# Four graph layers in fp32 on one core: the last layer's first matrix in 49 products for pairs of groups, and norms from accumulated sums

## The chip, the core and the metric

The kernel runs on one core of a Trainium2 chip. The metric is the device time of one execution in microseconds. Before the change it is 2160.31 us, the median of three runs (2158.48 to 2162.55). The profile is that of one further execution, whose span is 2156.5 us.

## What is computed

128 graphs of 64 nodes with 512 features pass through four layers. Each ends in x = layernorm(x + layer(x)), everything in fp32. Cut to what matters:

```python
# layer 0: scores s = (x @ w) @ a, A from tanh/exp of s_i + s_j and adj;  out = A @ x @ w
x = _layernorm(x + L0(x, adj, w, a))
# layer 1: weight = adj * exp(q @ k.T), rows normalised;                  out = weight @ v
x = _layernorm(x + L1(x, adj, Wq, Wk, Wv))
# layer 2: softmax over nodes of q . (adj @ k), times v
x = _layernorm(x + L2(x, adj, mask, Wqk, Wv))
# layer 3: two hypergraph convolutions
H = (adj != 0); Dn = 1 / (H @ adj[0]); Be = 1 / H.sum(axis=1)
conv(z, W, b) = Dn * (H @ (Be * (H.T @ (z @ W.T)))) + b
h = _layernorm(relu(conv(x, W1, b1)))      # W1: 1024 x 512
x = _layernorm(x + conv(h, W2, b2) + x)    # W2: 512 x 1024
```

(The last line stands for y + x inside the layer and x + layer(x) outside it.) gamma and beta of the inner norm are ones and zeros in the inputs, but the kernel folds them into W2 and its bias in general.

## The kernel before, in words

**Tiles and groups.** The 8192 nodes are 64 tiles of 128 rows (two graphs each). A group is two tiles, 256 nodes; there are 32 groups (`NG`). `run(g)` at L1005 writes down all steps of one group, 0 to 15: layer 0 in steps 0 to 2, layer 1 in 3 to 6, layer 2 in 7 to 11, layer 3 in 12 to 15. `prepare_chunk` (L700) makes the graph's small matrices for two groups at a time.

**Products by splitting.** A product of a group (256 rows) with a weight matrix is done as a 2x2 splitting with seven products in place of eight (`seven_products`, L849): the left side is cut into four blocks (`left_blocks`, L774), four sums of blocks are made on VectorE (`side_sums`, L829), and the weights exist as seven pieces in the order of `USE` (L488), four blocks and four sums less one that is not needed. Each of the seven results lies in a bank of PSUM; two banks go on accumulating, so that one product follows on the sum of earlier ones. `first` and `more` take a result out: with a scale from a column and added to x (`scaled_into`, L905), or copied. The first matrix of the last layer, called "3a" (512 x 1024), is such a product: the blocks have 128 rows, 256 of depth and 512 columns, so each of the seven products is two matmuls of 128x512 (L1125 to L1140). Its results are scaled, the bias b3a is added and they are summed in h on VectorE; relu follows on ScalarE. The second matrix, "3b" (1024 x 512), has seven products of four matmuls of 128x256 (L1148).

**Weights.** m1 and m2 stay in SBUF. The pieces of the others are computed once at the start, stored in DRAM (`stored_in_place`, L533) and for each group loaded again into the eight tiles of `ring` (`streamed`, L666), in loads of 512 KB.

**Norms.** `normalized` (L924) takes mean and variance of each tile with VectorE's batch statistics (`bn_stats`, `bn_aggr`), adds eps, raises to the power -0.5 on GpSimd, and applies scale and bias on ScalarE. Each group has four of them on x (512 columns) and one on h (1024).

**What sets the order.** No operation is emitted where it is written. `order.add` (L77) collects them with engine, planned cost, what they read and write, and a key. `keys_by_what_follows` (L106) sets the key from the group's place `BASE` (L29), and from the length of what follows in the group. `Order.run` (L141) then plays all engines through with planned costs (`w_pe`, `w_dve`, `w_act`, `w_pool`, L244 to L257) and latencies (`LATENCY`, L60): whenever an engine is free, it takes the ready operation with the lowest key for which buffers are free, and the instruction streams are written in that order. On TensorE, `choose` (L123) groups operations on the whole array and those on a divided array. The kinds of buffers at L299 to L311 bound what can be in flight: six x, fourteen `k4` of 4 KB a row, two h, eight banks, three `product` tokens. Every instruction is emitted through a wrapper, so the profile shows one line, L1177, for nearly all; its groups are told apart by the names of the tiles.

Of the kernel before, what the change touches and what calls it, by code (L numbers as in the profile page):

```python
# [16 lines left out]
P = 128  # L17
B, N, D, DH = 128, 64, 512, 1024
T = B * N // P
GT = 2  # L20
NG = T // GT
CT = 4
# [6 lines left out]
BASE = [APART * g - 2 * min(g, 4) - 2 * max(g - NG + 3, 0) for g in range(NG)]  # L29
# [25 lines left out]
class Op:  # L55
    __slots__ = ("engine", "cost", "emit", "key", "missing", "users", "takes", "touches", "start", "bytes", "step", "mode", "port", "behind", "group", "args", "matmuls")


class Order:
    LATENCY = {"PE": 220, "DVE": 70, "ACT": 60, "POOL": 60, "SP": 2200}  # L60
# [7 lines left out]
    EARLY = [2.22, 0.44, 0.0, 0.0, 0.0, 0.0, 0.0, 0.17, 0.0, 0.57, -0.17, -0.03, -1.1, -0.36, 0.0, -0.35]  # L68

    BLOCK, REST = 64, 3500  # L70
    AHEAD = 3.5

# [4 lines left out]
    def add(self, engine, cost, reads, writes, emit, urgent=0.0, size=0, mode=None, port=False, matmuls=0):  # L77
        o = Op()
        o.engine, o.cost, o.emit, o.key, o.step = engine, cost, emit, self.key - urgent - self.early, self.key
        o.start, o.mode, o.port, o.behind, o.group, o.args, o.matmuls = None, mode, port, None, self.group, (), matmuls  # L80
# [25 lines left out]
    def keys_by_what_follows(self):  # L106

        tail = {}
        for o in reversed(self.ops):
            if o.group is not None:  # L110
                own = 0 if o.engine == "SP" else 2 * o.cost if o.engine == "PE" else o.cost
                tail[o] = own + max((tail[u] + (u.engine != o.engine) * 3 * self.LATENCY[o.engine]
                                     for u in o.users if u.group == o.group), default=0)
        longest = max(tail.values())
        for o in reversed(self.ops):
            if o.group is not None:
                urgent = o.step - o.key
                o.step = BASE[o.group] + STEPS * (1 - tail[o] / longest)
                if o.engine == "SP" and o.users:
                    o.step = min(u.step for u in o.users)  # L120
                o.key = o.step - urgent

# [18 lines left out]
    def run(self):  # L141
# [11 lines left out]
        while len(done) < len(self.ops):  # L153
# [4 lines left out]
            for e, heap in ready.items():  # L158
                while free_at[e] <= now:
# [60 lines left out]
                    for u in found.users:  # L220
                        n += 1
                        heappush(events, (free_at[e] if u.engine == e and e != "SP" else seen, n, u, None))
# [25 lines left out]
def w_dve(n):  # L248
    return 175 + n * 35 // 32


def w_act(n):
    return 175 + n * 27 // 32
# [7 lines left out]
def kernel(  # L261
# [37 lines left out]
    kind("x", 6, GT, D)  # L299
# [7 lines left out]
    kind("k1", 2, CT, N)  # L307
# [3 lines left out]
    kinds["product"] = [None] * 3  # L311
# [12 lines left out]
    def dve(n, reads, writes, emit, urgent=0.0, port=None):  # L324

        if port is None:
            port = all((b[0] if isinstance(b, tuple) else b).kind != "bank" for b in reads)
        order.add("DVE", w_dve(n), reads, writes, emit, urgent, port=port)
# [184 lines left out]
    def in_dram(which, width):  # L513
        n = PIECE // width
        tiles = []
        for i in range(-(-len(USE) // n)):
            tiles.append(const(dram.tile([P, PIECE], FP, name=f"{which}_{i}"), n))
        stored[which] = [(t_, min(n, len(USE) - n * i)) for i, t_ in enumerate(tiles)]

        def store(k, piece):  # L520
            i = USE.index(k)
# [44 lines left out]

    def gram(name, left, right, steps):

        m = const(sb(name, len(USE), 2, D // 2), 2 * len(USE))
# [24 lines left out]
    m1 = gram("m1", wq1_raw, wk1_raw, KC)  # L594
    u1_c = const(sb("u1_c", KC))
# [30 lines left out]
    order.key = 3.0  # L626
    m2 = gram("m2", wq2_raw, wk2_raw, KC // 2)

    order.key = 6.0
# [16 lines left out]
    order.key = 8.0  # L646
    stored_in_place("3a", quarters(w3a), PIECE, PIECE)

    order.key = 10.0
# [16 lines left out]
    def streamed(which, room=()):  # L666

        pieces = []
        chunks = KH // 2 if which == "3b" else KC // 2
        for src, n in stored[which]:  # L670
# [5 lines left out]
                      urgent=1.5, size=P * n * width * 4)  # L676
            for k in range(n):
# [129 lines left out]
    def gathered(tokens, view, right, reads):  # L807
# [4 lines left out]
        def emit(t):  # L812

            for c in range(KC):
                for h, (rows, _) in enumerate(halves):
                    for f, (cols, _) in enumerate(halves):
                        at = (c * GT + t) * N
                        nc.tensor.matmul(ps[h].t[cols, at : at + N], view(t)[rows, c * P + f * N : c * P + f * N + N],
# [29 lines left out]

    def seven_products(a, s, pieces, first, more, across=False):  # L849


        going, pair = Buf("product"), [Buf("bank") for _ in range(2)]
        pieces = iter(pieces)

        def times(ps, left, start=True):
            piece, view = next(pieces)
            token = pair[ps] if isinstance(ps, int) else ps
            chunks = KH // 2 if left[2] else KC // 2
            width = PIECE // chunks if left[2] or wide else D // 2
# [14 lines left out]
            pe(w_pe(P, 2 * chunks) if across else w_pe(width, chunks), [left[0], piece, going], [token], emit,  # L874
# [3 lines left out]
        deep = a["deep"] if "deep" in a else False  # L878
        wide = a["wide"] if "wide" in a else False

        def side(v):
            return v[0], v[1], deep


        first("11", *times(0, side(a["11"])))
        first("22", *times(1, side(s[0])))
        more("11", *times(Buf("bank"), side(a["12"])))
        first("12", *times(0, side(s[1]), False))
        more("12", *times(1, side(s[3]), False))
        first("21", *times(Buf("bank"), side(a["22"])))  # L890
        u = times(0, side(s[2]), False)
        more("22", *u)
        more("21", *u)
# [11 lines left out]
    def scaled_into(at, f, own, n, base=None):  # L905


        def add(k, token, ps, base):
            dst = at[k]
            t = own.start + int(k[0]) - 1  # L910
            dve(n + 40, [*token, f, base[0]], [dst[0]], lambda: nc.vector.scalar_tensor_tensor(
                dst[1](), ps(), f.t[:, t : t + 1], base[1](), ALU.mult, ALU.add), NOW)

        return (lambda k, token, ps: add(k, token, ps, base[k] if base else at[k]),
                lambda k, token, ps: add(k, token, ps, at[k]))
# [8 lines left out]
    def normalized(reads_of, view, n_stats, eps, n, among=range(GT)):  # L924

        m = len(among)
        mv = Buf("col", m)
        for j, t in enumerate(among):
            st = Buf("col", n_stats)
            for i in range(n_stats):  # L930
                dve(n // n_stats, [reads_of(t, i)], [st[i]], lambda t=t, i=i, st=st: nc.vector.bn_stats(
                    st.t[:, 6 * i : 6 * i + 6], view()[:, t, ts(i, n // n_stats)]), port=False)
            dve(12, [st], [mv[j]], lambda j=j, st=st: nc.vector.bn_aggr(mv.t[:, 2 * j : 2 * j + 2], st.t[:, : 6 * n_stats]), port=False)
        ve, rstd, nm = Buf("col"), Buf("col"), Buf("col")

        def pairs_of(b, i):
            return b.t[:, : 2 * m].rearrange("p (t s) -> p t s", s=2)[:, :, i]

        dve(GT, [mv], [ve], lambda: nc.vector.tensor_scalar(ve.t[:, :m], pairs_of(mv, 1), eps, None, ALU.add))
        order.add("POOL", 790, [ve], [rstd],  # L940
                  lambda: nc.gpsimd.tensor_tensor(rstd.t[:, :m], ve.t[:, :m], mhalf[:, :m], ALU.pow), port=True)
        dve(GT, [mv, rstd], [nm], lambda: nc.vector.scalar_tensor_tensor(
            nm.t[:, :m], pairs_of(mv, 0), -1.0, rstd.t[:, :m], ALU.mult, ALU.mult))
        for j, t in enumerate(among):
            for i in range(n_stats):
                act(n // n_stats + 240, [reads_of(t, i), nm, rstd], [reads_of(t, i)], lambda j=j, t=t, i=i: nc.scalar.activation(
                    view()[:, t, ts(i, n // n_stats)], view()[:, t, ts(i, n // n_stats)], AF.Identity,
                    bias=nm.t[:, j : j + 1], scale=rstd.t[:, j : j + 1]))

    def layer_norm(xt, eps=EPS, among=range(GT)):  # L950
        normalized(lambda t, i: xt[[2 * t, 2 * t + 1]], lambda: xt.t, 1, eps, D, among)
# [53 lines left out]
    def run(g):  # L1005
# [9 lines left out]
        of_x = lambda t: xt[[2 * t, 2 * t + 1]], lambda t: xt.t[:, t, :]  # L1015
# [9 lines left out]
        for t in range(GT):  # L1025
# [13 lines left out]
        step(2)  # L1039
        seven_products(*left, first_use["w0"] if g == 0 else streamed("w0"), *scaled_into(  # L1040
            at_x, sums, slice(2 * CT + own.start, 2 * CT + own.stop), D // 2))
        layer_norm(xt)
# [11 lines left out]
        seven_products(*left, m1, *z_into(zT, u1_c), across=True)  # L1054
# [12 lines left out]
        po = [Buf("bank") for _ in range(GT)]  # L1067

# [7 lines left out]
        for t in range(GT):  # L1076
            dve(D + 40, [po[t], f, xt[[2 * t, 2 * t + 1]]], [xt[[2 * t, 2 * t + 1]]],
                lambda t=t: nc.vector.scalar_tensor_tensor(xt.t[:, t, :], po[t].t, f.t[:, t : t + 1], xt.t[:, t, :],
                                                   ALU.mult, ALU.add), NOW)
        layer_norm(xt)  # L1080
# [6 lines left out]
        seven_products(*left, m2, *z_into(zT2), across=True)  # L1087
# [21 lines left out]
        seven_products(*left, streamed("v2"), *scaled_into(at_x, wc, slice(0, GT), D // 2))  # L1109
        layer_norm(xt)  # L1110
# [14 lines left out]
        h = Buf("h", 4)  # L1125
        s3 = Buf("k1")
        a = left_blocks(gT3)
        at_h = block_views(h, lambda: h.t)

        def room(cell, i):  # L1130
            return (h[cell], lambda: h.t[:, cell // 2, ts(cell % 2 * 2 + i, D // 2)].rearrange("p (k q) -> p k q", q=P))

        s_ = [room(1, 0), room(1, 1),
              (s3, lambda: flat(s3.t).rearrange("p (k q) -> p k q", q=P)), room(2, 0)]
# [113 lines left out]
```

## Time and profile before

| what | value |
|---|---|
| median of three runs | 2160.31 us |
| span of the profiled execution | 2156.5 us, 3.8 us under that median |
| TensorE matmul busy | 2139.4 us |
| TensorE weight loads busy | 1721.0 us |
| VectorE, ScalarE, GpSimd busy | 1529.5, 861.1, 385.7 us |
| granted TensorE clock, mean | 0.999 |
| moved by DMA | 476.34 MB, mean 221 GB/s |
| TensorE idle, 0 to 76 us | 9.65 of 76 us |
| TensorE idle, 76 to 2136 us | 0.38 of 2060 us |
| TensorE idle, 2136 us to the end | 7.10 of 20.5 us |
| statistics of x (256 of 128x512) on VectorE | 175.0 us, 689 ns each |
| statistics of h (128 of 128x512) on VectorE | 87.3 us, 686 ns each |
| evictions into h (256 of 128x512) on VectorE | 95.4 + 93.1 us, 746 and 745 ns each |

The page names the engines PE (TensorE's matmuls), PEld (its weight loads), DVE (VectorE), ACT (ScalarE), POOL (GpSimd) and SP (the queue that issues DMAs). A row of digits gives the busy share in 40 slices of the span, in tenths. A group's row has the line, the engine, the operation, the tiles written and read, the shapes, the count, then busy time and the mean duration of one, then the idle time before its instructions and what ended it. Durations of matmuls overlap, so the mean of one is longer than the distance from one to the next; busy time divided by the count, or the distance in the timeline, is what one costs. A timeline row has the start, the length, the engine, the operation and how many instructions were merged.

### The profile page before, as it was taken

The numbers are of one execution on the slowest core, as the hardware profiler recorded it, in microseconds if no ns is written. First come the engines' busy times: TensorE is split into PE (matmuls) and PEld (weight loads), VectorE is DVE, ScalarE is ACT, GpSimd is POOL, SyncE is SP. The second block draws the span as 40 slices with busy tenths as digits, with TensorE's granted clock in tenths as the row PEclk, the third lists the DMA queues.
The fourth block names the chain that finished last, engine by engine and source line by source line (L and its number), as shares of the span: only waits on it lengthen the run. The fifth ranks groups of instructions, "written<-read, shape, count | busy, mean of one in ns | idle before, by whom it ended". The sixth has DMA issues, their size and how long they took to land.

```text
span 2156.5 us, 51432 instructions
## 1 busy us (share of the span) xinstructions
PE 2139.4 (99%) x20829; PEld 1721.0 (80%) x20829; DVE 1529.5 (71%) x3967; ACT 861.1 (40%) x1812; POOL 385.7 (18%) x399
## 2 busy tenths in 40 slices
PE   8999999999999999999999999999999999999998
PEld 4988777787887887878878887888888788888866
DVE  6787767677776676767777776767766777766675
ACT  3444344343343434343443344443434434433343
POOL 1112122011211212111122111212012220112030
PEclk9999999999999999999999999999999999999999
DMA  8775667676666656665666766667666666665576
GB/s 284 268 276 206 229 209 258 227 240 216 218 223 218 207 202 228 220 229 194 211 225 215 228 212 200 215 215 233 220 202 215 221 205 225 213 203 200 171 246 209
DMA packets 174365, 476.34 MB, mean 221 GB/s; under 512 B 35825, under 2 KB 45361, under 8 KB 174129
## 3 DMA queue, kind: packets, MB, share of 16 engines
q1 hardware_dynamic: 174128, 473.05, 66.0%
q8 instruction: 165, 2.70, 0.5%
q14 instruction: 72, 0.58, 0.1%
HBM read 443.33 MB, written 29.66 MB: 219 GB/s over the span
## 4 chain that ended last, share of the span: by engine, by line
PE 97%; DMA 2%; DVE 0%; SPq 0%; ACT 0%; issue 0%; DVEq 0%; ACTq 0%
PE bank L1177 97%; DMA x<-in_x_dram 0%; DMA k<-in_wk_dram 0%; DMA mask_rows<-e 0%; DMA k<-in_wqk_dram 0%; DMA ring<-in_wv_dram 0%; DMA ring<-w 0%; SPq L1177 0%; DVE x L1177 0%; DVE col L1177 0%; DVE ring L1177 0%; ACT x L1177 0%; DVE e L1177 0%; ACT k L1177 0%; DVE k L1177 0%
## 5 line engine op out<-in xcount | busy, mean ns | idle before, releaser
L1177 PE MATMUL bank<-ring,k 128*128 128x256 f32 (+1 forms) x3968 | 1027.7, 409 | 2.3 <-DMA ring<-w 1.5
L1177 PEld LDWEIGHTS bank<-ring,k 128*128 128x128 f32 x3968 | 732.3, 190 | 205.5 <-issue 115.0
L1177 ACT COPY k<-bank 128x512 f32<-128x512 f32 (+1 forms) x640 | 304.3, 501 | 599.0 <-PE bank L1177 513.3
L1177 DVE SCALAR_TENSOR_TENSOR x<-bank,col,x 128x256 f32<-128x256 f32 (+1 forms) x832 | 399.8, 500 | 195.0 <-PE bank L1177 181.3
L1177 PEld LDWEIGHTS bank<-k,m 128*128 128x128 f32 x3584 | 432.8, 192 | 30.5 <-issue 19.9
L1177 PE MATMUL bank<-k,m 128*128 128x128 f32 x3584 | 445.9, 276 | 0.0
L1177 PE MATMUL bank<-ring,h 128*128 128x256 f32 (+1 forms) x1408 | 421.8, 440 | 0.0
L1177 POOL TENSOR_TENSOR col<-col,mhalf 128x2 f32<-128x2 f32 (+1 forms) x161 | 111.4, 692 | 1347.6 <-DVE col L1177 668.9
L1177 PEld LDWEIGHTS bank<-ring,h 128*128 128x128 f32 x1408 | 255.8, 191 | 73.4 <-issue 48.6
L1177 ACT ACTIVATE x<-x,col,col 128x512 f32<-128x512 f32 x256 | 197.7, 809 | 240.6 <-DVE col L1177 237.8
L1177 DVE TENSOR_TENSOR k<-bank,k 128x256 f32<-128x256 f32 x384 | 153.3, 420 | 100.0 <-PE bank L1177 95.9
L1177 DVE BATCH_NORM_STATS2 col<-x 128x6 f32<-128x512 f32 x256 | 175.0, 689 | 11.0 <-ACT e L1177 5.4
L1177 DVE SCALAR_TENSOR_TENSOR h<-bank,col,b3a_b 128x512 f32<-128x512 f32 x128 | 95.4, 746 | 56.0 <-PE bank L1177 55.5
L1177 DVE TENSOR_TENSOR k<-k 128x256 f32<-128x256 f32 x226 | 94.8, 420 | 54.1 <-ACT k L1177 54.0
L1177 ACT ACTIVATE h<-h 128x512 f32<-128x512 f32 x128 | 80.2, 632 | 104.4 <-DVE h L1177 104.0
L1177 DVE SCALAR_TENSOR_TENSOR h<-bank,col,h 128x512 f32<-128x512 f32 x128 | 93.1, 745 | 37.8 <-PE bank L1177 37.0
L1177 ACT ACTIVATE h<-h,col,col 128x512 f32<-128x512 f32 x128 | 94.5, 804 | 58.0 <-DVE col L1177 58.0
L1177 POOL TENSOR_TENSOR k<-k,b3b_b 128x512 f32<-128x512 f32 x64 | 81.2, 1269 | 196.6 <-ACT k L1177 81.1
L1177 ACT ACTIVATE k<-bank,u_c 128x128 f32<-128x128 f32 x256 | 82.0, 366 | 82.4 <-PE bank L1177 80.8
L1177 PEld LDWEIGHTS bank<-k,k 128*64 128x64 f32 (+1 forms) x2112 | 77.1, 140 | 46.1 <-issue 20.5
L1177 PE MATMUL bank<-k,k 128*64 128x64 f32 (+1 forms) x2112 | 105.1, 237 | 5.9 <-DMA k<-in_wk_dram 4.6
L1177 DVE BATCH_NORM_STATS2 col<-h 128x6 f32<-128x512 f32 x128 | 87.3, 686 | 20.2 <-ACT h L1177 20.0
(96 smaller groups left out, 1489.2 us busy)
## 6 DMA issues: line engine op xcount, KB each, us to landing
ring<-3a SPq DMA_DIRECT2D x224, 512.0 KB, 4.5
ring<-3b SPq DMA_DIRECT2D x224, 512.0 KB, 4.3
ring<-v SPq DMA_DIRECT2D x189, 512.0 KB, 3.7
ring<-w SPq DMA_DIRECT2D x93, 512.0 KB, 3.4
x<-in_x_dram SPq DMA_DIRECT2D x32, 512.0 KB, 4.0
ring<-v SPq DMA_DIRECT2D x63, 256.0 KB, 4.0
out_dram<-x SPq DMA_DIRECT2D x31, 512.0 KB, 3.7
ring<-w SPq DMA_DIRECT2D x31, 256.0 KB, 4.8
```

What stands on the lines that cost most here:

```text
L1177: made = f(*args, **kwargs)
```

## The change

**A second splitting for 3a.** Groups go in pairs (`SG = 2`). `run(g)` now ends before the product with 3a and puts its group on a list; `run_rest` takes two groups from it and does steps 12 to 15 for both. The pair's 512 rows are split 2x2 with sums as before (`pair_left_side`, blocks of 256 rows), and each of the seven products is split 2x2 once more (`forty_nine_products`): `inner_sums` makes four more sums of the left blocks, and each inner product is one matmul of 128 rows, depth 128 and 256 columns, 49 in all. The 49 pieces of weights are made at the start from the seven (`stored_twice`): seven loads, 21 subtractions on VectorE and 7 on GpSimd, 49 stores. Each outer product's result is put together in a `k4` tile f by three copies on ScalarE and three sums on VectorE from two banks; five sums of 1024 columns on VectorE and two on GpSimd put the seven f into the two h. The two h of the pool are now both used by one pair. Scale and bias of h come afterwards in one operation of 1024 columns a tile.

**Groups alone.** For the first and the last pair (`APART_3A`) each group goes on by itself with seven products of 3a.

**One stream of 3b.** `products_of` runs the seven products with 3b for both groups of a pair on each piece of weights, so the pieces are loaded once a pair.

**Norms.** The last instruction that writes x also accumulates its row sum (`accum_out`); ScalarE squares x less its mean and accumulates that (a scratch tile takes the squares); relu accumulates the row sums of h. The batch statistics go.

**The planner.** `BASE` becomes a list of 32 fitted numbers; costs, latencies and EARLY are changed; the wait of an engine on its own results is counted (`AGAIN`); what follows is measured over the pair; one x more, one kind (`k1`) less, two `product` and two `inner` tokens in place of three `product`. The start's preparations have new keys (`PREPARED`): m2 at -1.85 (was 3.0), v2 at 7.399 (6.0), 3a at 8.218 (8.0), 3b at 15.311 (10.0).

The diff, cut to its core:

```diff
-BASE = [APART * g - 2 * min(g, 4) - 2 * max(g - NG + 3, 0) for g in range(NG)]
+BASE = [
+    0.0, 1.743, 3.491, 5.253, 9.791, 13.561, 18.091, 21.891, 26.391, 30.191, 34.691, 38.491, 42.991, 46.791, 51.291, 55.091,
...
+APART_3A = (0, NG // SG - 1)
+PREPARED = [-1.85, 7.399, 8.218, 15.311, 12.896, -0.62]
...
-    LATENCY = {"PE": 220, "DVE": 70, "ACT": 60, "POOL": 60, "SP": 2200}
+    LATENCY = {"PE": 210, "DVE": 125, "ACT": 140, "POOL": 120, "SP": 2200}
+    AGAIN = {"PE": 0, "DVE": 115, "ACT": 115, "POOL": 120}
+    TO_PE = 100
...
-    kind("x", 6, GT, D)
+    kind("x", 7, GT, D)
...
-    kind("k1", 2, CT, N)
...
-    kinds["product"] = [None] * 3
+    kinds["product"] = [None] * 2
+    kinds["inner"] = [None] * 2
...
+    def inner_products(raw, room, at, which, pieces, f, width):
...
+        def times(bank, i, k, start=True):
+            piece, view = next(pieces)
+            token, left = side(k)
+            def emit():
+                nc.tensor.matmul(bank.t[:, ts(i, width)], left(), view()[:, 0], start=start, stop=True, skip_group_check=True)
+            pe(w_pe(width), [token, piece, going], [bank, *([y_] if k == "11" else [])], emit, matmuls=1)
...
+        times(x_, 1, "11")
+        times(x_, 0, "0", False)
+        into([1, 2], x_, 0, 2, True)
+        times(y_, 0, "12")
+        times(x_, 1, "1", False)
+        times(x_, 0, "3", False)
+        into([0], x_, 1, 1, True)
+        into([0], x_, 0)
+        times(y_, 1, "22", False)
+        times(x_, 1, "2", False)
+        into([3], x_, 1, 1, True)
+        into([1], x_, 1)
+        into([2, 3], y_, 0, 2)
...
-                dve(n // n_stats, [reads_of(t, i)], [st[i]], lambda t=t, i=i, st=st: nc.vector.bn_stats(
-                    st.t[:, 6 * i : 6 * i + 6], view()[:, t, ts(i, n // n_stats)]), port=False)
...
+            junk = Buf("k4" if n == DH else "k2")
+            act(n + 240, [cells(t), nm], [q[j], junk], lambda j=j, t=t, junk=junk: nc.scalar.activation(
+                like(junk.t[:, :n], view(t)), view(t), AF.Square, bias=nm.t[:, j : j + 1], accum_out=q.t[:, j : j + 1]))
...
+        def use(name, f_):
+            f = kept[name] = f_, lambda: f_.t
+            if name == "2":
+                add(h_block(0, 0), kept["1"], f)
+            elif name == "6":
+                add(f, kept["1"], f, pool)
+                add(h_block(0, 1), f, kept["5"])
+            elif name == "3":
+                add(h_block(0, 1), h_block(0, 1), f)
+            elif name == "7":
+                add(f, kept["6"], f, pool)
+                add(h_block(1, 0), f, kept["4"])
+                add(h_block(1, 1), f, kept["5"])
...
+        if n == SG:
+            forty_nine_products(gT3, *left, streamed("3a"), DH // 4, use)
+        else:
+            seven_products({**left[0], "wide": True}, left[1], streamed("3a1"), first, more)
...
+        products_of(sides, streamed("3b"))
...
+        if len(waiting) == SG or g // SG in APART_3A:
+            run_rest(len(waiting))
```

More of the change, by code (lines that the diff above doesn't have):

```diff
@@ L21 @@
 NG = T // GT
+SG = 2
+TOK = GT * P
 CT = 4
@@ L1144, in run @@
[L1144 to L1154 removed]
+        waiting.append((g, xt, gT3, in_g, own, dc, dh))
```

379 lines of the change are left out of this document (279 added, 100 removed).

## The prediction

> **What bounds the kernel now.** I read the page from the top: the busy shares, the slices, the chain that ended last.
>
> ```profile
> span 2156.5 us, 51432 instructions
> ...
> PE 2139.4 (99%) x20829; PEld 1721.0 (80%) x20829; DVE 1529.5 (71%) x3967; ACT 861.1 (40%) x1812; POOL 385.7 (18%) x399
> ...
> PE   8999999999999999999999999999999999999998
> ...
> DVE  6787767677776676767777776767766777766675
> ...
> PE 97%; DMA 2%; DVE 0%; SPq 0%; ACT 0%; issue 0%; DVEq 0%; ACTq 0%
> ```
>
> TensorE is busy from the second slice to the last, the chain is 97% TensorE, and no other engine is above 71%. A busy matmul row can hide gaps, so I next looked at the spacing of matmuls in the TensorE timeline of the middle of the run. (One fp32 matmul of the code is two instructions of the trace, so counts there are double.)
>
> ```profile
> 1003.21 7.07 PE L1177 MATMUL bank<-ring,k 128*128 128x256 f32 x32
> ...
> 1032.52 1.89 PE L1177 MATMUL bank<-ring,h 128*128 128x256 f32 x8
> ...
> 1045.63 2.84 PE L1177 MATMUL bank<-k,m 128*128 128x128 f32 x24
> 1048.31 1.88 PE L1177 MATMUL bank<-ring,h 128*128 128x512 f32 x4
> 1050.12 1.15 PE L1177 MATMUL bank<-k,k 128*64 128x64 f32 x32
> ...
> 1055.05 1.05 PE L1177 MATMUL bank<-k,m 128*128 128x128 f32 x8
> 1055.94 1.88 PE L1177 MATMUL bank<-ring,h 128*128 128x512 f32 x4
> 1057.66 5.31 PE L1177 MATMUL bank<-ring,k 128*128 128x512 f32 x12
> ```
>
> 24 more instructions of 256 columns take 7.07 - 1.89 = 5.18 us, 216 ns each; 8 more of 512 take 3.43 us, 429 ns each. So a matmul costs 432 ns at 256 columns and 858 at 512, in proportion to its columns. The stages' table gives a granted clock of 1.00 from 0 to 2136 us. The grouped rows, whose means hold every gap, give the upper figures:
>
> ```profile
> L1177 PE MATMUL bank<-ring,k 128*128 128x256 f32 x3456 | 798.6, 382 | 2.3 <-DMA ring<-w 1.5 <-DVE k L1177 0.6 <-ACT k L1177 0.2
> ...
> L1177 PE MATMUL bank<-ring,h 128*128 128x256 f32 x1024 | 241.1, 381 | 0.0
> L1177 PE MATMUL bank<-ring,k 128*128 128x512 f32 x512 | 232.1, 593 | 0.0
> ...
> L1177 PE MATMUL bank<-ring,h 128*128 128x512 f32 x384 | 180.9, 595 | 0.0
> ```
>
> Busy over count: (798.6 + 241.1) / 2240 matmuls = 464 ns, (232.1 + 180.9) / 448 = 922 ns. The 32 and 64 ns above the dense spacing are switches and waits. The kernel is bound by TensorE's columns; a change is worth what it takes from them, unless it opens gaps.
>
> **Columns removed.** All 512-column matmuls of the table belong to the first matrix of the last layer: 7 products of 2 matmuls per group. For a pair that is 28, or 28 x 858 = 24.02 us. The 49 products of one 256-column matmul each are 49 x 432 = 21.17 us. The gain is 2.86 us a pair. 14 pairs do so; the groups of the first and the last pair keep seven products. Sum: **-40.0 us**; by the grouped rows, 28 x 922 - 49 x 464 = 3.08 us a pair, -43.1 us. I take the dense spacing, since gaps need not fall with the columns. The 56 products of a pair in the second matrix stay as they are: only their weights are read once instead of twice.
>
> **Boundaries.** A product is now released on one matmul, where it was on two of 512. If each inner product carried the 64 ns of a 512 row, 14 x (49 - 28) x 64 ns = +18.8 us. But the 32 instructions at 1003.21 are eight products of two matmuls, and they too follow at 216 ns: a boundary whose operands are ready costs nothing there. I take 0 and keep +19. Set against that, the two instruction orders hold 260 changes between whole and divided array before and 230 after. The timeline shows such a change at 1050.1 us, where 4 x 429 ns from 1048.31 leave 0.09 us: -3 us, with 0 as the other end.
>
> [...]
>
> **VectorE.** Removed, from the grouped rows: statistics 175.0 + 87.3, their aggregation 38.9 + 9.2, evictions into h 95.4 + 93.1, the 256-column side sums of h 41.2: 540 us. Added per pair: 14 evictions of 256 (420 ns) and 7 of 512 (some 690: the same sum in SBUF takes 686), 12 inner sums of 256 (420) and 4 of 128 (285), 4 outer sums of 512 (690), 5 sums of 1024 (1334): 26.3 us, 368 in 14 pairs. The scale of h in 1024s (746 + 2 x 267 = 1280 ns, by the 256 and 512 rows) is 82; 448 reads of accumulated sums at 82 ns are 37; some 254 more column operations at 160 ns are 41; the rest 20. 548 against 540: VectorE stays near 1540 us. All of it lies beside TensorE. Cover: the instruction order spreads a pair's 49 products over some 36 us of TensorE work, with 71 operations there and 68 of VectorE. But its 26.3 us exceed the 21.2 of the products they serve, so without other groups' matmuls it would bind; see the rivals.
>
> **ScalarE.** Removed: relu 80.2 and scale 94.5. Added: 256 squares of 512 columns, which no row shows; the nearest ACTIVATEs take 632 (relu) and 809 ns (scale and bias from columns). At 720, 184 us. The 1024 forms take 432 ns more (372 to 588 ns for 256 columns more, twice): 64 x (1.06 + 1.15 + 1.24) = 221. Copies out of the banks: 196 x 0.372 + 98 x 0.588 + 16 x 0.588 = 140. Reading 384 sums: between 0 and 0.2 us each, 31 us at VectorE's 82 ns. Together 861 + 400, some 1260 us, 60%. Hidden beside TensorE; ScalarE's own largest wait is 594.1 us for TensorE's banks. Were Square to need another table, each switch would cost the 1283 ns of the one ACT_TABLE_LOAD; the changed program holds one load, so no. **GpSimd** gains 28 sums of 2364 ns, 66 us on 18%: hidden.
>
> **DMA.** 98 issues of 512 KB of 3b go, about 51 MB; 3a per pair shrinks from fourteen tiles to twelve and a quarter. Added once: 7 loads of 512 KB and 49 stores of 128 KB, some 10 MB, 34 us at the 300 GB/s of the start. The first pair does not need them, and the DMA share after 76 us is 0.66. I take 0, bounds -5 (weights of layer 2 come earlier, where TensorE idles 9.7 us of 76) and +6. **End:** the last norm exchanges 0.69 + 0.18 us of statistics for two column operations and a square, 0.16 + 0.16 + 0.75, for two tiles: +1 us.
>
> **Late evictions.** The product's bank is written again after its ScalarE copy and VectorE sum. In the new order one to three matmuls of other operations stand between nearly all of these steps, but VectorE has some 29 us of work in those 36. I take +3, between 0 and the 19 above.
>
> Sum: -40 - 3 + 0 + 1 + 3 = -39 on a span of 2156.5 us, that is 2117.5. The profiled span lies 3.8 us under the median of 2160.31; with it, **2121 us**.
>
> **Rivals.** (a) Half the gain: the +18.8 of boundaries comes in full, or evictions are late by 0.2 us in each of the 98 inner products (+20): 2121 + 19 = 2140. For it: three rounds bank, copy, bank in each product; against: the idle list of TensorE before has 10 us in all, with 1568 products released the same way. (b) Slower: VectorE binds while the 49 products run. Place: the bank of an inner product. Price: if nothing else filled the gaps, 26.3 - 21.2 = 5.1 us a pair, 71 us: 2121 + 71 = 2192. It decides from 2.9 us of waiting a pair. For it: 29 us of VectorE in 36; against: the interleaved order and 71% before without a wait. (c) More gain: grouped rows' -43 and half the other gaps closed by the new order. The 32 ns of 2240 matmuls alone are 72 us, of which 10 to 15 could go: 2105.
>
> **Chances.** Forecast, 2108 to 2132: 0.58. Rival (a), to 2156: 0.18. Rival (c), below 2108: 0.14. Slower (b): 0.10. The range leaves out (b) and the far ends of (a) and (c): 2104 to 2144, also the bounds of the unknown costs. About 0.2% is what a measurement of this kernel can tell from no change (2158.48 to 2162.55 in three runs); the narrow strip within it takes 0.02 from (a): faster 0.88, same 0.02, slower 0.10.
>
> **What would show it.** The last layer's 512-column matmuls fall from 448 to 56 (112 instructions), those of 256 rise by 686, still 216 ns apart; PE stays at 99%; VectorE near 72%, ScalarE near 60%; no row "PE bank <- DVE k" above some 10 us. Rival (a) shows as a spacing above 225 ns in inner products, (b) as idle TensorE released by VectorE and VectorE at 90% in stretches of 36 us. I would be wrong if the squares or pairs delay the norm of h past the 19 us of other matmuls that the order puts behind the last inner product.

## The result and the profile after

The kernel became slower by 0.5%: **2169.52 us**, median of five runs (2167.43 to 2175.61), against 2159.68 us for the kernel before in five runs (2158.48 to 2162.55). The ratio is 1.0047 with a 95% interval of 1.0035 to 1.0060. The forecast of 2121 us, its range up to 2144 us and its sign are all wrong. The profiled execution took 2169.41 us with a span of 2167.3 us, 10.8 us over the span before; the sums below explain these 10.8.

The page of the kernel after, its busy shares, TensorE's row of slices and the chain that ended last:

```profile
span 2167.3 us, 54072 instructions
...
PE 2118.1 (98%) x21467; PEld 1839.7 (85%) x21467; DVE 1489.6 (69%) x4346; ACT 1205.9 (56%) x2698; POOL 455.2 (21%) x434
...
PE   8999999999999999999999999999999999999998
...
PE 95%; issue 1%; DMA 1%; DVE 1%; ACT 1%; SPq 0%; POOLq 0%; DVEq 0%; ACTq 0%
```

TensorE was busy for 21.3 us less than before (2139.4), so something was gained; its idle time rose from 17.1 to 49.2 us. VectorE and ScalarE are below what was forecast. The grouped rows of TensorE say what went and what came:

```profile
L1459 PE MATMUL bank<-ring,k 128*128 128x256 f32 x4828 | 1130.2, 383 | 4.1 <-ACT k L1459 2.5 <-DMA ring<-w 0.3
...
L1459 PE MATMUL bank<-ring,h 128*128 128x256 f32 x1024 | 233.1, 381 | 0.0
L1459 PE MATMUL bank<-kept,h 64*64 64x64 f32 x4096 | 78.4, 226 | 24.8 <-issue 24.8
...
L1459 PE MATMUL bank<-ring,k 128*128 128x512 f32 x112 | 50.2, 594 | 1.6 <-ACT k L1459 1.6
```

The three rows of `ring` hold the matmuls with streamed weights: 1130.2 + 233.1 + 50.2 = 1413.5 us where it was 1452.7. The row `kept,h` is the 64x64 matmuls on a divided array that gather h over the graph's edges at the start of step 14 (`gathered`, L875; 16 of the code, 32 of the trace, an operation). The change does not touch their number, 4096. Yet 24.8 us of idle time now stand in front of them, with no releaser: "issue" is time in which the engine waited for nothing that the profile shows. The list of TensorE's waits has the same on top (us in total, times, longest):

```profile
PE bank L1459 <- issue: 25.9, 14, 2.8
PE bank L1459 <- DMA k<-in_wk_dram: 4.8, 2, 4.2
PE bank L1459 <- ACT e L1459: 4.5, 3, 3.7
PE bank L1459 <- ACT k L1459: 4.1, 5, 1.6
```

A row's busy time merges overlaps, so I added the time from each matmul's start to the next one's start; this account has no remainder. In us:

| matmuls | before | after | h_left_out | fitted_again |
|---|---|---|---|---|
| with streamed weights (`ring`) | 1381.3 | 1354.6 | 1349.8 | 1357.8 |
| gathers of h (`kept,h`) | 66.4 | 98.0 | 67.6 | 72.4 |
| all others, and ends | 708.8 | 714.7 | 712.9 | 713.7 |
| span | 2156.5 | 2167.3 | 2130.3 | 2143.9 |

(The last two columns are experiments, below.) In `ring`, 1372 more instructions of 256 columns at 216 ns are +296.4 us and 784 fewer of 512 at 429 ns are -336.3: **-40.0**, as forecast. The other 13.3 us of `ring` came back: 6.1 of them in the first 76 us, 6.7 later and 0.5 at the end. The gathers of h cost **+31.6**, the others +5.9 (mostly small matmuls next to the gathers: `row_of,e` +2.9, `bh,kept` +2.2, `ones,adj` +1.2). -40.0 + 13.3 + 31.6 + 5.9 = +10.8.

The timeline of TensorE shows what happens to the gathers in eleven of the fourteen pairs (start, length, what, number, idle before):

```profile
332.15 9.66 PE L1459 MATMUL bank<-ring,k 128*128 128x256 f32 x44
341.74 1.15 PE L1459 MATMUL bank<-k,k 128*64 128x64 f32 x32
...
343.34 0.65 PE L1459 MATMUL bank<-kept,h 64*64 64x64 f32 x32
343.81 1.04 PE L1459 MATMUL bank<-k,e 64*64 64x512 f32 x8
344.78 0.38 PE L1459 MATMUL bank<-row_of,e 128*128 128x2 f32 x2
345.09 2.20 PE L1459 MATMUL bank<-kept,h 64*64 64x64 f32 x133
349.52 0.65 PE L1459 MATMUL bank<-kept,h 64*64 64x64 f32 x26 [2.23 <-issue]
...
350.29 2.12 PE L1459 MATMUL bank<-kept,h 64*64 64x64 f32 x60
352.34 7.89 PE L1459 MATMUL bank<-ring,k 128*128 128x256 f32 x33
```

Between two blocks of large matmuls stand some 10 us of small ones alone. The first 133 of the long run follow at 16 ns, then TensorE stands still for 2.23 us in the middle of an operation; the matmul that goes on has no wait for another engine in its record. So I suspected that the next instruction was missing. The trace has loads of instructions too, as DMAs of 16 KB (queue q8 of the page: 169, 2.77 MB). Set beside the standstills they say the same in every case: all fourteen end 2.3 to 2.5 us after such a load began (in the one shown, the load starts at 347.2 us and TensorE goes on at 349.5), while two loads are on average some 13 us apart. Three of the long runs have a second standstill, and 127, 127 and 128 matmuls stand between the two; by the estimate in the last section, one load holds some 127 matmuls with their weight loads. In the kernel after, the 17 closest pairs of loads are 3.4 to 3.7 us apart; in the kernel before none are nearer than 4.3 us.

Before, the same gathers stood 32 to 96 at a time (once 128) between large matmuls:

```profile
331.73 1.03 PE L1177 MATMUL bank<-ring,k 128*128 128x256 f32 x4
...
332.80 1.16 PE L1177 MATMUL bank<-kept,h 64*64 64x64 f32 x64
333.89 10.87 PE L1177 MATMUL bank<-ring,k 128*128 128x256 f32 x40
...
365.87 1.63 PE L1177 MATMUL bank<-kept,h 64*64 64x64 f32 x96
367.43 2.00 PE L1177 MATMUL bank<-ring,h 128*128 128x256 f32 x8
```

In the whole order, uninterrupted runs of divided-array matmuls had at most 128 instructions before (once; all others 104 or fewer). After, 24 runs have 128 or more, ten of them 204 to 228; those ten took 71.6 us for 2064 instructions, 35 ns each. (Such a run holds other small matmuls besides the gathers: the 82 runs of 90 to 109 instructions in the kernel before took 23 ns each.) The stages from the standstill on also show the granted clock (stretch, its length, busy time and instructions of PE, PEld, DVE, ACT, POOL, then the clock, the DMA share and GB/s):

```profile
344.50:349.50 5.00, 2.79 (x139) 2.36 (x135) 4.27 (x13) 3.28 (x8) 0.00 (x0) 1.00 0.90 339
349.50:352.30 2.80, 2.78 (x95) 2.71 (x95) 0.54 (x3) 1.62 (x5) 0.00 (x0) 0.59 0.07 24
352.30:356.00 3.70, 3.70 (x17) 3.18 (x16) 2.10 (x6) 2.65 (x7) 0.69 (x1) 0.85 0.00 0
```

After the standstill TensorE's granted clock is 0.50 for 3.41 us (349.98 to 353.40 us), and the work behind it is slower too: in such stretches matmuls of 256 columns of `ring` start 427 ns apart (median of twelve distances), where it is 216 at the full clock. The records hold five such stretches in the middle of the kernel after and none in the middle of the kernel before.

**Why the order has such runs.** The planner's `choose` puts at most 64 matmuls of the code (128 of the trace) of a divided array into 3.5 us, but only as long as an operation on the whole array is ready beside them; without one it returns what there is. In the pair's stretch none is: the 49 products finish the h of both groups at about the same time, and the second matrix now waits for both (`products_of` takes both on one piece of weights), so the gathers of h of both groups fall due together with nothing large behind them. (That is read from the code and the timeline; no run tried the two parts of it one by one.) My **theory** from here on: runs of small matmuls longer than the supply of instructions allows cost 30 to 40 us, and that is the missing gain. The **rival**: the new norms, with longer chains through ScalarE and VectorE, make TensorE late.

### The profile page after: what moved, and what is told of

Its sections match the earlier page's. It is cut to its first block, busy times and chain, and to the rows that moved or that the text cites. A ratio compares the mean times of both kernels' runs of the same rounds, so it can differ in the third digit from the quotient of the medians.

```text
span 2167.3 us, 54072 instructions
## 1 busy us (share of the span) xinstructions
PE 2118.1 (98%) x21467; PEld 1839.7 (85%) x21467; DVE 1489.6 (69%) x4346; ACT 1205.9 (56%) x2698; POOL 455.2 (21%) x434
## 3 DMA queue, kind: packets, MB, share of 16 engines
q8 instruction: 169, 2.77, 0.5%
## 4 chain that ended last, share of the span: by engine, by line
PE 95%; issue 1%; DMA 1%; DVE 1%; ACT 1%; SPq 0%; POOLq 0%; DVEq 0%; ACTq 0%
PE bank L1459 95%; ACT k L1459 1%; DVE k L1459 1%; DMA k<-in_wk_dram 0%; DMA adj<-mask_rows 0%; SPq L1459 0%; DMA ring<-w 0%; DMA adj<-in_adjT_dram 0%; DVE h L1459 0%; ACT e L1459 0%; ACT h L1459 0%; DVE x L1459 0%; DVE col L1459 0%; DVE ring L1459 0%; ACT m L1459 0%
## 5 line engine op out<-in xcount | busy, mean ns | idle before, releaser
L1459 PE MATMUL bank<-ring,k 128*128 128x256 f32 x4940 | 1178.3, 388 | 5.7 <-ACT k L1459 4.1
L1459 PEld LDWEIGHTS bank<-ring,k 128*128 128x128 f32 x4940 | 909.0, 191 | 154.4 <-issue 23.5
L1459 ACT COPY k<-bank 128x512 f32<-128x512 f32 (+1 forms) x934 | 429.2, 484 | 485.0 <-PE bank L1459 378.6
L1459 PEld LDWEIGHTS bank<-k,m 128*128 128x128 f32 x3584 | 434.2, 192 | 13.3 <-DVE col L1459 1.3
L1459 DVE TENSOR_TENSOR k<-bank,k 128x256 f32<-128x256 f32 (+1 forms) x678 | 296.7, 459 | 182.5 <-PE bank L1459 140.1
L1459 ACT ACTIVATE k<-x,col 128x512 f32<-128x512 f32 x256 | 184.2, 722 | 189.9 <-DVE col L1459 188.9
L1459 PE MATMUL bank<-ring,h 128*128 128x256 f32 x1024 | 233.1, 381 | 0.0
L1459 DVE TENSOR_TENSOR k<-k 128x256 f32<-128x256 f32 (+1 forms) x349 | 145.5, 432 | 47.0 <-ACT k L1459 45.8
L1459 DVE TENSOR_TENSOR k<-k,k 128x256 f32<-128x256 f32 (+3 forms) x361 | 176.6, 493 | 0.5
L1459 POOL TENSOR_TENSOR x<-x,bv_b 128x512 f32<-128x512 f32 x64 | 81.3, 1274 | 272.9 <-PE bank L1459 233.0
L1459 PE MATMUL bank<-kept,h 64*64 64x64 f32 x4096 | 78.4, 226 | 24.8 <-issue 24.8
L1459 DVE TENSOR_SCALAR col<-col 128x2 f32<-128x2 f32 (+2 forms) x402 | 72.6, 190 | 40.1 <-ACT k L1459 33.9
```

The source lines that it names most:

```text
L1459: made = f(*args, **kwargs)
```

## The experiments

**h_left_out**: of each gather of h, half of the matmuls are left out (the second 64 features of each chunk), everything else and the order stay.

```diff
-                    for f, (cols, _) in enumerate(halves):
+                    for f, (cols, _) in enumerate(halves[:parts]):
```

(`parts` is 1 for h and 2 elsewhere.)

> The changed kernel in its own order, with half of the matmuls in the gathers of h left out (of each 16 in an operation, the 8 for the second half of the features; the output is not the reference's), the others in the old 64x64 form. The gathers of h take 66 us of TensorE in the kernel before and 98 us in the changed one. Theory (instruction supply): the 33 us of the matmuls left out go, and the 32 us of starved time with them, and the stretches at half clock behind it: 2169.5 - 33 - 32 - 8 = 2097 us (2090 to 2107), no idle stretch without a releaser. Rival (TensorE waits for other engines' results and the idle only shows there): what is left out is 33 us at most, and part of it turns into waiting: 2136 to 2150 us.

2133.36 us, ratio 0.9877 (0.9861 to 0.9892). The same place of the timeline:

```profile
339.92 1.15 PE L1459 MATMUL bank<-k,k 128*64 128x64 f32 x32
...
343.26 2.48 PE L1459 MATMUL bank<-kept,h 64*64 64x64 f32 x77
...
346.88 8.04 PE L1459 MATMUL bank<-ring,k 128*128 128x256 f32 x36
```

7.0 us instead of 10.6, with no standstill here; waits for "issue" fall from 25.9 to 1.8 us in all, and no stretch at half clock is left in the middle. The account's column has the gathers at 67.6 us, as before the change. That is *not* less work of theirs: half as many now cost 33 ns each, where 16 ns is the price in the kernel before, so 2048 of them need what 4096 needed. Of the 37.0 us that the span lost against after, 30.4 are in the gathers; the rest is in the work around them, but for 1.4 us of `ring` in the first 76 us, which lie ahead of all gathers of h. The expected number was missed, because it took a share for the left-out matmuls themselves, and the time lies between theory (2090 to 2107) and rival (2136 to 2150). So it is the trace that decides, not the time: the standstills and the half clock go, and no wait for VectorE or ScalarE comes in their place (`ACT k` 4.1 us in after, 4.3 here).

**half_h** keeps the results and halves the number of instructions: one matmul with a left side of 64x128 in place of two of 64x64, in all gathers of h. **half_all** does so in all gathers.

```diff
+                    if wide:
+                        nc.tensor.matmul(ps[h].t[:, at : at + N], view(t, rows, c * P, P), right(h, t), start=True, stop=True)
+                        continue
```

> The changed kernel, with the order of all operations and every result as they are, but the gathers of h take a left side of 64 rows by 128 columns in one matmul where two of 64x64 stood: 8 matmuls an operation in place of 16. Theory (instruction supply): in the changed kernel the gathers of a pair stand in one run of some 150 small matmuls, the 16 KB loads of TensorE's instructions come 3.5 us apart there, and TensorE runs dry once a pair (14 idle stretches of 1.2 to 2.8 us with no releaser, 28 us, and 5 stretches of 3.4 us at half clock behind them). With half the instructions the run needs no more loads than come: the idle stretches before gathers of h go, time about 2130 us (2124 to 2142). Rival (late evictions and norms: TensorE waits for VectorE's and ScalarE's results, the idle stretches are only where this shows): nothing that it waits for comes earlier, so 2165 to 2172 us.

> As half_h, with the gathers of x halved too (64x128 left sides in all gathers). Theory (instruction supply): the run that stalled is already cured by the gathers of h, so within 4 us of half_h, about 2128 us; if the 64x128 form takes longer on TensorE than two of 64x64, it is slower than half_h by that, 512 operations of x. Rival (late evictions): 2165 to 2172 us.

2191.36 us (1.0140, 1.0123 to 1.0157) and 2247.18 us (1.0401, 1.0385 to 1.0416): both missed. In half_h the "issue" waits are gone, the clock is back at 0.997, and this row tells what went wrong:

```profile
L1462 PE MATMUL bank<-kept,h 64*128 64x64 f32 x2048 | 125.3, 274 | 0.0
```

2048 instructions take 121.9 us from start to start, 60 ns each; the two that each replaces cost 32. So the cure cost 121.9 - 66.4 = 55.5 us. The same price shows in half_all for the gathers of x (36.5 to 63.8 and 33.9 to 62.8 us). These runs agree with a starved supply (half the instructions, no standstill) and prove nothing by their times.

**half_in_four** uses the form in half of a pair's eight gather operations.

> The changed kernel in its own order, with the 64x128 left sides of half_h in only four of the eight gathers of h of each pair (the second tile of each). The form itself costs 0.217 us an operation (55.5 us in 256 operations of half_h): 56 x 0.217 = 12 us. Theory (instruction supply): a pair's run has 32 matmuls less, so of 36 us of starved time some 23 go, and most half clock: 2169.5 + 12 - 23 - 5 = 2154 us (2148 to 2160). Rival (TensorE waits for other engines): 2181 us.

2170.85 us (1.0053, 1.0039 to 1.0067), no better than after. Gathers of h take 105.0 us, 7 more than in after; the other rows gain as much. I had priced the form at half of what it costs: half_h has 128 operations on h (four in each of 32 groups), not 256, so one costs 55.5 / 128 = 0.434 us and 56 cost 24 us, not 12. With that price the same sum gives 2169.5 + 24 - 23 - 5 = 2166 us, 5 under the measured time: the price of the form and the relief about cancel.

**norms_alone** has no pairs and no 49 products (every group takes seven products), the old `BASE` and `EARLY`, but all else of the change. **planner_alone** is the kernel before with only the planner's new costs, latencies and its rule for an engine's own results.

```diff
-APART_3A = (0, NG // SG - 1)
+APART_3A = range(NG // SG)
```

> The changed kernel with every group by itself (seven products of 3a, 3b streamed for each group) and with the places in time and the early starts of the kernel before: what is left of the change is the norms from accumulated sums, the planner's new costs and latencies, and the way h is scaled afterwards. Theory (instruction supply): no pair, so no run of 128 gathers; no idle stretch of over 1 us in the middle, matmul work as before, 2155 to 2168 us. Rival (the new norms are late): idle TensorE released by ScalarE or VectorE, or many gaps of 0.1 to 0.5 us, and over 2175 us.

> The kernel before with the changed kernel's planned costs, latencies and rule for an engine's own results, and nothing else of the change (batch statistics, no pairs, the old places in time). Against norms_alone (2175.4 us), which differs by the norms from accumulated sums and the scaling of h afterwards. If the new norms cost the 14 us of norms_alone: 2155 to 2165 us. If the planner's constants cost them: 2170 to 2180 us.

2175.40 us (1.0068, 1.0053 to 1.0083) and 2158.24 us (0.9993, 0.9984 to 1.0002). The planner's costs do nothing. norms_alone is 17 us above planner_alone without any wait for "issue" (gathers of h 67.7 us), outside the range of the theory and in that of the rival. I first read that as the price of the new norms, and as 17 us of after. The next runs took this reading apart.

**short_squares** (after) and **norms_short_squares** (norms_alone) square only the first 64 columns of each row; the order stays, the variances are those of 64 columns.

```diff
-                like(junk.t[:, :n], view(t)), view(t), AF.Square, bias=nm.t[:, j : j + 1], accum_out=q.t[:, j : j + 1]))
+                junk.t[:, :64], view(t)[:, :64] if n == D else view(t)[:, 0, :64], AF.Square, bias=nm.t[:, j : j + 1], accum_out=q.t[:, j : j + 1]))
```

> The changed kernel in its own order, with the variance taken from the first 64 columns of each tile only (a square of 64 columns in place of 512 or 1024; the output is not the reference's). ScalarE has 0.35 to 0.8 us less in each of 320 squares. If the squares on ScalarE, which stand in the chain of each norm, are what holds TensorE: 2150 to 2160 us. If the starved run of small matmuls is (32 to 36 us, untouched by this): 2163 to 2170 us.

> norms_alone with the same cut of the squares. It was 17 us slower than planner_alone (2175.4 against 2158.2), which has batch statistics. If the time of the squares makes that difference: 2157 to 2164 us. If it is the order that the planner writes with the longer chain (which is the same here): 2170 to 2176 us.

2169.40 us (1.0042, 1.0027 to 1.0057) and 2175.79 us (1.0059, 1.0041 to 1.0078): no change in either. The time of the squares on ScalarE is hidden, as forecast.

**no_norms_alone** is norms_alone with batch statistics in every norm (of h in four pieces of 256 columns, where the kernel before takes two of 512); **norms_h_alone** has them for x only. **pairs_statistics** and **pairs_statistics_x** are the same two edits in the kernel after, with its pairs.

```diff
-        normalized(lambda t: xt[[2 * t, 2 * t + 1]], lambda t: xt.t[:, t, :], sums, parts, eps, D, among)
+        by_statistics(lambda t: xt[[2 * t, 2 * t + 1]], lambda t: xt.t[:, t, :], lambda t: [lambda: xt.t[:, t, :]], eps, D, among)
```

> No pairs and batch statistics in all norms; what is left of the change are the planner's costs, the copy of h with its scale afterwards (1024 columns in one operation) and the seventh x. If the norms cost the 17 us: 2157 to 2163. Rival, the later scale of h or the buffers cost them: 2171 to 2176.

> The kernel with the new norms and no pairs, but batch statistics for the norms of x; only h by accumulated sums. With everything new it took 2175.4 us, with none of the norms 2158.2. If the norms of x cost the 17 us: 2158 to 2163; if that of h: 2171 to 2176; if both, in between.

> The kernel after with its pairs, 49 products and fitted keys, but the norms of x and of h by VectorE's batch statistics as before (h in four pieces of 256 columns a tile; no accumulated sums, no squares). If the new norms cost the pairs the 17 us that they cost the kernel without pairs (2175.4 against 2158.2): 2149 to 2158, with the idle 'issue' time of 26 us still there. Rival: the 17 us are a matter of the order without pairs only, or the 250 us of VectorE that come back (from 1490 to some 1740 us, 80%) hold TensorE in the 49 products: 2167 or more.

> The kernel after, batch statistics for the norms of x alone; h keeps accumulated sums and squares. If the cost sits in the four norms of x, which have the least work behind them to wait beside: as the kernel with all statistics, 2149 to 2158. If it sits in the norm of h (a square of 1024 columns and a scale ahead of it): 2165 to 2171.

2177.14 us (1.0076, 1.0061 to 1.0091), 2170.42 (1.0048, 1.0033 to 1.0063), 2247.18 (1.0400, 1.0385 to 1.0416) and 2187.71 (1.0129, 1.0109 to 1.0150). The rival, that the new norms cost the time, falls twice. norms_h_alone lies where both kinds of norm would share the 17 us, but no_norms_alone speaks against that: without pairs, the old norms are as slow as the new ones, so the 17 us belong to something that those kernels share: the later scale of h, the tokens and buffers, or the preparations' order; which, stays open. With pairs, both times lie above their ranges for that case (2149 to 2158): the old norms are 18 us (x) and 78 us (all) *slower* than the new. The waits of pairs_statistics say why:

```profile
PE bank L1484 <- DVE x L1484: 32.8, 12, 3.8
PE bank L1484 <- ACT k L1484: 23.3, 18, 2.1
PE bank L1484 <- ACT h L1484: 10.6, 11, 3.0
```

With VectorE at 1691.5 us, 76%, TensorE waits for it and for what stands behind it. That comes near to rival (b) of the prediction, in the kernel that does not have the new norms; but the waits are for VectorE's work on x, and the row that (b) named, `DVE k`, has 0.2 us here too. (The keys were fitted to the new norms, so some of the 78 us may be the order's.) And the 17 us are no part of after: in norms_alone they sit in `ring` (+6.5 us against planner_alone), the 128-column products `k,m` (+7.2) and the 64-column `k,k` (+2.2), while after has `k,m` at 405.7 against 404.6 us before and these `k,k` at 69.4 in both.

**before_clumped**: the kernel before, with the planner's limit on small matmuls switched off.

```diff
-    BLOCK, REST = 64, 3500
+    BLOCK, REST = 64, 0
```

> The kernel before, with the one rule taken out that keeps small matmuls apart (at most 64 in 3.5 us): every instruction is there, in an order with runs of up to 100 and more small matmuls, and whole-array work is left without cover more often (some 35 us by the plan). Theory (instruction supply): beside those 35 us another 30 to 40 us of idle TensorE without a releaser, in many pieces, and stretches at half clock: 2225 us or more. Rival: 2195 us, and the idle time has other engines as releasers.

2207.13 us in one run, between theory and rival, with 13.5 us of "issue" waits that the kernel before does not have (its eight standstills of over 1 us all end 2.2 to 2.4 us after an instruction load began), but also 30.0 us of waiting for x from ScalarE, which the other order brought. Gathers of h rose only from 66.4 to 73.6 us. It shows the standstills in the old kernel, and not their price.

**fitted**: all instructions of after; the planner now adds the lateness of small matmuls beyond 64 in 3.5 us to its own clock, may begin them earlier, and `BASE` is fitted again under that.

```diff
-                        began += [now + turn + found.cost * i // found.matmuls for i in range(found.matmuls)]
+                        for i in range(found.matmuls):
+                            at = now + turn + found.cost * i // found.matmuls
+                            late = max(0, began[-self.BLOCK] + self.REST - at)
+                            turn += late
+                            began.append(at + late)
```

> The changed kernel with every instruction, only in another order: the planner counts a late start when more than 64 small matmuls would start within 3.5 us, may go to a divided array while whole-array work is still there, and the places of the groups in time are fitted again with that. Theory (instruction supply): no idle stretch without a releaser, no half clock in the middle; the changed kernel without its 32 us of starved time and 8 us of half clock, 2122 to 2145 us, faster than the kernel before. Rival (late evictions and norms): the same waits, 2165 us and more.

2160.02 us (1.0000, 0.9992 to 1.0009), 9.5 us under after, where 24 to 47 were expected: missed. "issue" fell to 6.3 us and the gathers of h to 78.0 us, 20 less; the other rows together gave 8 back (`k,m` and `e,same` some 3 each) (the work is cut into more pieces: 306 changes between whole and divided array, 232 in after).

**fitted_again**: the same with 0.09 us more for ScalarE's accumulating instructions, the 64x128 form only where the planner finds it cheaper (three operations, at the halved price of half_in_four), and a new fit.

> The fitted order once more, with two things added: the planner takes the 64x128 form for a gather where that costs less than the late start, and counts 0.09 us more for a ScalarE instruction that accumulates. Against fitted (2160.0 us) the plan is 4 us shorter. If the planned costs now hold what fitted missed, 2140 to 2152 us; if fitted missed something else (its time lies 48 us over its plan, the kernel before 21 over its own), 2153 to 2163 us.

**2145.73 us**, ratio **0.9926 (0.9913 to 0.9938)**: 15 us under the kernel before, 24 under after, as expected. The same products, norms and pairs, in another order; its busy shares and the top of its waits:

```profile
PE 2118.5 (99%) x21369; PEld 1834.5 (86%) x21369; DVE 1472.7 (69%) x4346; ACT 1206.1 (56%) x2698; POOL 457.2 (21%) x434
```

```profile
PE bank L1479 <- issue: 4.8, 5, 1.6
PE bank L1479 <- ACT e L1479: 4.6, 3, 3.7
```

TensorE's busy time is that of after; 24 us of idle time have gone. Which of the three steps brought the 14 us against fitted was not tried. No run of small matmuls has more than 136 instructions, and no half clock is left in the middle.

## Why the prediction was wrong, point by point

- **Columns, -40.0: right.** The counts changed as forecast, and the dense spacings of 216 and 429 ns stayed.
- **Boundaries, 0 with +19 kept: right on the whole.** What `ring` has above its columns rose from 21.7 to 28.4 us between the first 76 us and the end, and 3.4 of these 6.7 go away in h_left_out. Rival (a) did not come.
- **Turns, -3: the step that failed.** I read 230 changes in place of 260 between whole and divided array as a small gain. Fewer changes for the same small matmuls means longer runs of them, and without a word I carried the 16 ns that a gather cost in the old, short runs over to these. A gather cost 24 ns after the change (98.0 us for 4096): TensorE stood still in these longer runs, 24.8 us of "issue" in front of gathers; that it lacked instructions there is my theory. The term that is missing from the sum is +31.6 us in the gathers of h, and with the half clock and the small matmuls beside them some 36 us (h_left_out). The order, which I counted for this, and the planner's limit of 64 in 3.5 us, which stands in the kernel, both pointed at it.
- **Norms, squares and evictions hidden: right**: short_squares shows it for the squares, and waits for VectorE's and ScalarE's sums outside the start are 4.7 us. VectorE 1489.6 us for 1540, ScalarE 1205.9 for 1260, GpSimd 455.2 for 452: the first two were sized too high. My closing doubt, the norm of h, was not what happened.
- **Rival (b), slower because VectorE binds: right sign by luck, wrong mechanism.** Its row, `DVE k`, is 0.3 us in after. TensorE waited long for VectorE only with the old norms.
- **Load time of the weights**, no term of the sum: PEld rose from 1721.0 to 1839.7 us, 85%, and large matmuls still follow at 216 ns.
- **DMA, 0, from -5 to +6:** TensorE's waits for DMAs fell from 7.4 to 5.1 us, and TensorE's idle time in the first 76 us is the same, 9.7 us. But 3.7 of it are now one wait at 43.8 us for a tile `e` of ScalarE, which itself waits 3.5 us for VectorE, and half clock follows (0.54 from 47.4 to 53.5 us; 6.8 us in all, which by estimate lose half of that, 3.4 us). So of the 6.1 us that `ring` lost there, some only moved over from other rows. I had only priced DMAs at the start. What makes that chain late was not tried.
- **End, +1:** idle time in the last 20 us went from 7.1 to 7.9 us.

In sum: -40.0 for the columns was there. With the waits for "issue" down to 1.8 us, in h_left_out, 13.8 us of it are missing in the account: 8.5 in `ring` (4.8 of them in the first 76 us), 4.1 in the other rows and 1.2 in the gathers; what makes these up is open in part. The standstills in the long runs, with what follows them, make up most of the other 37.0: -40.0 + 13.8 + 37.0 = +10.8.

## What to carry to other kernels

Price small instructions by the length of the run they will stand in, not by their mean in the old order (a gather took 16 ns there and 24 in the new one): count, in the new order, how many follow each other without a large one between. Taking two groups through one product and one stream of weights also lets their small work fall due at the same time. And a part run alone in a list-scheduled kernel is another order: its time says something of the whole only if the rows that rose are the same.

## What the runs showed of the hardware

- **TensorE stood still in long runs of small matmuls.** In runs of 64x64 matmuls at 16 ns it did so fourteen times in the kernel after, for 1.1 to 2.8 us, with no releaser, after 22 to 176 matmuls of the run, and each time it went on 2.3 to 2.5 us after the start of an instruction load. That it had run out of instructions is a reading of these times; no record says so.
- **Instruction loads.** The page's queue q8, "instruction", has 169 packets of 16 KB, 2.77 MB, in the kernel after; over its 2 x 21467 matmuls and weight loads that is 64.5 bytes each (165 packets, 2.70 MB over 2 x 20829 before; 154 in h_left_out, where 2 x 2048 were left out). If all of them are TensorE's, which the profile does not say, a load is by estimate some 127 matmuls with their weights. In the run shown two loads stand 3.5 us apart, at 347.2 and 350.7 us, where by the same estimate 127 x 16 ns = 2.0 us of work is in each. What sets the 2.3 to 2.5 us and the 3.5 us (the DMA share was 0.90 from 344.5 to 349.5 us) stays open.
- **Half of the gathers of h took as long as all.** With the second 64 features of each chunk left out, 2048 matmuls of 64x64 took 67.6 us, 33 ns each (h_left_out); all 4096 took 66.4 us, 16 ns each, in the kernel before. What makes this so was not tried.
- **One wide left side was dearer than two narrow ones**: 60 ns for 64x128 (half_h), 32 for two of 64x64 (before).
- **Some standstills of 2 us were followed by a lower clock.** Of seven of 2.0 to 2.8 us in the kernel after, five were followed by 3.41 us at a granted clock of 0.50, and two (2.4 and 2.1 us) were not. The wait of 3.7 us at the start was followed by 6.83 us of it.
- **An accumulated sum on ScalarE is an instruction of its own in the trace of after**: each square is followed by a read of the accumulator, 193 ns on average for the 256 on x, 49.5 us in all. With those on h it is 384 reads and 73.9 us, where the prediction counted 31.
